# Cross-attention of a two-block kernel: softmax with queries on partitions before the transposes, in place of sums by products with ones after them

## The chip, the cores and the metric

The kernel runs on one core of one Trainium2 chip. The metric is the device time of one execution in microseconds (us); the times of a kernel are given as the median of its runs. The engines are called PE (TensorE, with PEld for its weight loads), DVE (VectorE), ACT (ScalarE), POOL (GpSimd) and SP (SyncE, which issues most DMAs). Each works through its own queue in order.

## The reference

Two transformer blocks run one after the other on x of 2 batches x 1024 tokens x 256 features, in float32. Both have self-attention over the 1024 tokens, then cross-attention over a context of 64 rows per batch, then a feed-forward part: in the first block a mixture of 8 experts of which each token uses 2, in the second a plain one. There are 16 heads of 16 features. The part that matters here is cross-attention, the same in both blocks but for biases and a mask:

```python
q = heads(norm(x) @ q_w.T)            # 1024 queries of a batch, 16 heads
k = heads(context @ k_w.T)            # 64 keys
v = heads(context @ v_w.T)
scores = einsum('bhqd,bhkd->bhqk', q, k) * 0.25   # block 2 adds a bias by the mask
attn = softmax(scores, axis=-1)
out = merge(einsum('bhqk,bhkd->bhqd', attn, v))
x = x + out @ proj_w.T
```

## The kernel before, in words

**Stages.** Each block (layer 0 and 1) begins with the first batch's norm and heads, then runs 128 *cells* (the loop at L954): one cell computes 4 tiles of scores for the maxima ahead (kind "a", L801, reduced by DVE at L808) and 4 tiles of scores again with the maxima folded in (kind "b", L812, exponentiated by ACT at L818), and every second cell multiplies the exponentials by the values (L863), which ACT copies (L875) and POOL adds up (L876). Eight PSUM banks go round for everything on PE: `bank()` (L230) takes the one that has been free longest, and a matmul waits until the bank's earlier reader is done. In the last 10 cells there are no more "a" scores; the flag `maxima[0]` then turns False, and `helper()` (L310) gives DVE in place of POOL.

**The order of the work.** A `Stream` (L131) holds all the other work as generators: norms, projections, cross-attention, the experts' dispatch and slots. Every task yields its estimated PE time in us, or zero or a negative number: wait until the next cell, or for that many us. In the cells `step` takes the able task with the earliest deadline and then the highest rank, as far as a budget of us for the cell goes. After the cells `rest` (L178) plays the remaining tasks against these estimates: the highest rank that isn't waiting goes next. All this happens while the program is written; on the chip the order is fixed on each engine.

**Cross-attention.** For each of 4 *units* of 512 queries in a layer, 8 in all, `cross_tasks` (L1071) adds three tasks: a norm (rank 67 or 40), `weigh` (rank 30, estimated at 17 us) and `share` (rank 50), which projects the result and adds it to x. The next unit's norm waits for this unit's `weigh`. `weigh` (L1098) first projects the queries (L1108). Its unit has 2 groups g of 8 heads, each of 4 tiles r; a tile holds 2 heads for the 512 queries: 128 queries on partitions, and along the free axis 4 such blocks of queries, each with 2 heads x 64 keys. Its steps are:

- `scores` (SC, L1123), two tiles at once: PE products (L1138; in layer 1 also the mask's, L1129). With `maxima` on, ACT copies the tile to SBUF (L1149); else DVE takes the maximum over each 64 keys (L1158) and subtracts it (L1159) straight from PSUM.
- `largest` (LA, L1164), with `maxima` on: the maximum by DVE (L1158) and the subtraction by POOL (L1159) in SBUF.
- `weights_turned` (TU, L1168), two tiles: 4 transposes each on PE (L1174), then Exp by ACT from PSUM to SBUF (L1178). From here on keys are on partitions.
- `product` (PR, L1184), once per g: the values' products (L1187), then 16 small products with ones, held in `picks` at O_SUM (L1197), which give the sums over keys; ACT copies the values' result (L1204) and DVE inverts the sums (L1206).
- `divided` (DI, L1209): 4 products with `picks` at O_HEAD spread the inverses over the features (L1212), and DVE multiplies (L1219). For g = 1 this is done in `share`, between waits of 2.6 and 1.2 us.

The order of these steps is written out by hand, once for units within the cells (L1227, 11 steps with a yield of 0.0 after each while `maxima` is on) and once for units after them (L1250, waits in us). A unit that begins within the cells keeps the first list, with its own waits once `maxima` is off.

**What goes on around the tails.** A unit of layer 0 is followed by a dispatch task (rank 70), which routes its tokens to experts and writes them to DRAM; `find` and `rows` then make the numbers of the experts' 20 slots, and `Mixture.slot` (rank 10 less the slot's number, estimated at 14.4 us) runs a slot's two matrix products with Gelu (L1657) between. Slot 0 can run after two units, slots 1 to 4 after the third, the others after the fourth. At the end of layer 0's cells the pools of its self-attention are closed and, in their place on the right side of SBUF, pools are opened in this order: `kpool`, `slotw` (slots' weights), `epool` 0 and 1 (slots' activations). Layer 1's beginning runs beside the slots (`beside`, L1981). After layer 1's cells, `forward_task` (rank 0, 28 us for each of 4 blocks, Gelu at L1814) runs in what the cross-attention leaves.

Of the kernel before, what the change touches and what calls it, by code (L numbers as in the profile page):

```python
# [106 lines left out]
O_SUM, O_HEAD = 0, 128  # L107

O_ROWS, O_PART = 640, 704
NPICK = 768  # L110
# [91 lines left out]
def two_blocks(  # L202
# [100 lines left out]
    def other_constants():  # L303
        nc.gpsimd.memset(restart, 1.0)
        nc.gpsimd.memset(restart[:, :, 0:1], 0.0)
        nc.gpsimd.memset(vbds[0], 0.0)

# [214 lines left out]
    def self_attention(layer, tail, heads, arrive, extra, when_ready, beside=None):  # L522
# [379 lines left out]
        if layer == 0:  # L902
            norm_pairs(0, TB, ln, x_turned(0), f"{names}0", arrive)

            one = small.tile([P, 1], F32, tag="one", name="one", bufs=1)
            nc.vector.tensor_copy(one, cols[:, C_ONE : C_ONE + 1])
            fill_heads(range(NK), one)
            other_constants()
            prepare()
            for i in range(2):  # L910
                spread_bias(i)
            for _ in first_heads():
                pass
# [184 lines left out]
    def weigh(layer, b, pool, w, name, held):  # L1098
# [68 lines left out]

        def weights_turned(g, n):  # L1168

            for r in (2 * n, 2 * n + 1):  # L1170
                i, p = bank()
                sc = less.pop((g, r))
                for t in range(4):
                    nc.tensor.transpose(  # L1174
                        p[:, t * P : (t + 1) * P], sc[:, t * P : (t + 1) * P], ident
                    )
                pt = pts[g, r] = pool.tile([P, 512], F32, tag="p1", name=f"pt_{name}{g}{r}", bufs=4)
                nc.scalar.activation(pt, p, AF.Exp, scale=SCALE)  # L1178
                free.append(i)


        inverse = {}

        def product(g):  # L1184
# [9 lines left out]
            j, s = bank()  # L1194
            for r in range(4):
                for c in range(4):
                    nc.tensor.matmul(  # L1197
                        s[32 * c : 32 * (c + 1), :P],
                        lhsT=picks[:, O_SUM + 32 * r : O_SUM + 32 * (r + 1)],
                        rhs=pts[g, r][:, c * P : (c + 1) * P],  # L1200
                        start=(r == 0),
                        stop=(r == 3),
                    )
            nc.scalar.copy(q[:, g, :], o)  # L1204
            inv = inverse[g] = pool.tile([P, P], F32, tag="inv", name=f"inv_{name}{g}", bufs=2)
            nc.vector.reciprocal(inv, s[:, :P])  # L1206
            free.extend((i, j))

        def divided(g):  # L1209
            i, p = bank()  # L1210
            for c in range(4):
                nc.tensor.matmul(  # L1212
                    p[:, c * P : (c + 1) * P],
                    lhsT=picks[:, O_HEAD + c * P : O_HEAD + (c + 1) * P],
                    rhs=inverse[g],
                    start=True,
                    stop=True,
                )
            nc.vector.tensor_tensor(q[:, g, :], q[:, g, :], p, ALU.mult)  # L1219
            free.append(i)  # L1220

        held.update(ot=q, divided=divided)
        cost = 1.9 if layer else 1.0
        SC, LA, TU, PR, DI = scores, largest, weights_turned, product, divided
        if maxima[0]:

            for now, wait in (  # L1227
                (((SC, 0, 0), (LA, 0, 0)), 0.0),
                (((LA, 0, 1),), 0.0),
                (((SC, 0, 1), (LA, 0, 2)), 0.0),  # L1230
                (((TU, 0, 0), (LA, 0, 3)), 0.0),
                (((SC, 1, 0), (LA, 1, 0)), 0.0),
                (((TU, 0, 1), (LA, 1, 1)), 0.0),
                (((SC, 1, 1), (LA, 1, 2)), 0.0),
                (((PR, 0), (LA, 1, 3)), -1.5),
                (((TU, 1, 0),), None),
                (((DI, 0), (TU, 1, 1)), -1.4),
# [4 lines left out]
                us = sum({SC: cost, TU: 1.15, PR: 1.1, DI: 0.55}.get(step[0], 0.0) for step in now)  # L1242
# [7 lines left out]
        for step, *args, wait in (  # L1250
            (SC, 0, 0, None),
            (SC, 0, 1, -1.0),
            (TU, 0, 0, None),
            (SC, 1, 0, None),
            (TU, 0, 1, -1.3),
            (PR, 0, None),
            (SC, 1, 1, None),
            (TU, 1, 0, None),
            (DI, 0, None),
            (TU, 1, 1, -1.6),  # L1260
            (PR, 1, None),
        ):
            step(*args)
            yield {SC: cost, TU: 1.15, PR: 1.1, DI: 0.55}[step]
# [716 lines left out]
    def beside(begin):  # L1981
# [4 lines left out]
        both.rest({}, 0)  # L1986
        mixture.others()
# [18 lines left out]
def _layout(inputs):  # L2006
# [84 lines left out]
    for r in range(4):  # L2091
        for u in range(2):
            for c in range(4):
                picks[SK * u : SK * (u + 1), O_SUM + 32 * r + 8 * c + 2 * r + u] = 1.0
# [52 lines left out]
```

## Time and profile before

| what | value |
|---|---|
| median of 3 runs | 1614.07 us (1609.81 to 1619.12) |
| the profiled execution: time | 1624.94 us |
| its span, first to last instruction | 1623.2 us |
| mean granted PE clock | 0.985 of full speed |
| Exp and Gelu table loads on ACT | 12, and one of another function at the start, 1283 ns each |

The profile is of one execution. Its page gives each engine's busy time, the chain of work that ended last, followed back from the end, and groups of like instructions by source line. Its windows give busy time by stretch of the span: layer 0's cells run from about 80 to 590 us, the experts' slots to about 950, layer 1's cells to about 1465, and the last feed-forward blocks to the end. An L with a number is a line of the kernel before. PE busy times are from modelled ends, so that neighbours seem to overlap by about 0.1 us.

### The profile page before, as it was taken

How to read it: one execution, taken by the hardware profiler on the slowest of the kernel's cores; microseconds unless marked ns; L12 is line 12 of the kernel's file. 1: busy time of each engine (PE TensorE's matmuls, PEld its weight loads, DVE VectorE, ACT ScalarE, POOL GpSimd, SP SyncE). 2: the span in 40 equal slices, each digit the busy share in tenths (PEclk: the TensorE clock that was granted, in tenths of full speed). 3: DMA queues.
4: the chain of work that ended last, by engine and by line, in shares of the span. 5: the costliest groups of instructions: out<-in, count | busy, mean ns of one | idle time of the engine just before them, and what ended most of it. 6: DMA issues, size and time to landing. Idle time of an engine off the chain costs nothing.

```text
span 1623.2 us, 28319 instructions
## 1 busy us (share of the span) xinstructions
PE 1579.5 (97%) x10710; PEld 876.8 (54%) x10710; DVE 985.1 (61%) x2094; ACT 912.9 (56%) x1767; POOL 411.0 (25%) x546
## 2 busy tenths in 40 slices
PE   7999999999998999999999999999999999999998
PEld 3433444544443547878888653344344435546766
DVE  5787776687778647511114457876867767855400
ACT  3487777676665755332233327876776676674321
POOL 2243323144235202311112032411322323311000
PEclk9899999999998999999999999999999999999999
DMA  5235311101000115375556321101110002000000
GB/s 158 112 133 194 111 27 34 28 21 47 14 21 34 54 50 196 102 275 188 186 201 217 92 72 27 33 23 21 34 33 21 22 14 83 15 14 21 14 13 26
DMA packets 55751, 121.07 MB, mean 75 GB/s; under 512 B 12218, under 2 KB 26428, under 8 KB 55228
## 3 DMA queue, kind: packets, MB, share of 16 engines
q1 hardware_dynamic: 51772, 109.07, 20.7%
q0 software_dynamic: 3456, 9.51, 1.6%
q8 instruction: 86, 1.41, 0.4%
q10 hardware_dynamic: 384, 0.66, 0.2%
q14 instruction: 53, 0.43, 0.1%
HBM read 71.68 MB, written 38.88 MB: 68 GB/s over the span
## 4 chain that ended last, share of the span: by engine, by line
PE 89%; DVE 7%; ACT 1%; issue 1%; DMA 1%; another core or an unknown queue 1%; POOL 0%; SPq 0%; DVEq 0%; POOLq 0%; ACTq 0%
PE banks L812 16%; PE banks L801 14%; PE banks L863 13%; PE banks L1651 8%; PE banks L1681 8%; PE banks L631 4%; PE banks L433 3%; PE banks L1823 3%; PE banks L1811 3%; DVE mx_s L808 3%; PE banks L1138 2%; PE banks L601 2%; PE banks L1174 2%; PE banks L1108 2%; PE banks L365 2%; PE banks L709 1%
## 5 line engine op out<-in xcount | busy, mean ns | idle before, releaser
L808 DVE TENSOR_REDUCE mx_s<-banks 128x1 f32<-128x512 f32 x1024 | 634.7, 682 | 215.3 <-PE banks L801 210.3
L818 ACT ACTIVATE pt_s<-banks 128x512 f32<-128x512 f32 x1024 | 532.6, 609 | 155.7 <-PE banks L801 124.8
L801 PE MATMUL banks<-KS,QS 16*128 16x512 f32 x2048 | 537.4, 631 | 4.0 <-DVE count L1441 2.6
L812 PE MATMUL banks<-qb_s,KS 32*128 32x512 f32 x2048 | 517.6, 623 | 6.7 <-DVE qb_s L711 3.7
L876 POOL TENSOR_TENSOR acc_s<-acc_s,part_s 128x512 f32<-128x512 f32 x141 | 179.5, 1273 | 439.0 <-ACT part_s L875 438.3
L812 PEld LDWEIGHTS banks<-qb_s,KS 32*128 32x128 f32 x2048 | 181.0, 187 | 178.5 <-DVE mx_s L808 105.4
L863 PE MATMUL banks<-pt_s,v_s 128*20 128x512 f32 x2048 | 262.0, 603 | 1.5 <-DVE mx_s L808 1.0
L801 PEld LDWEIGHTS banks<-KS,QS 16*128 16x128 f32 x2048 | 200.9, 186 | 76.3 <-issue 37.0
L1681 PE MATMUL banks<-w_slot,h_s 128*128 128x256 f32 x640 | 143.3, 380 | 2.7 <-ACT h_s L1657 2.7
L863 PEld LDWEIGHTS banks<-pt_s,v_s 128*20 128x20 f32 x2048 | 43.0, 98 | 185.0 <-ACT pt_s L818 131.6
L1681 PEld LDWEIGHTS banks<-w_slot,h_s 128*128 128x128 f32 x640 | 120.5, 190 | 22.8 <-ACT h_s L1657 3.1
L875 ACT COPY part_s<-banks 128x512 f32<-128x512 f32 x155 | 92.7, 598 | 61.3 <-PE banks L863 50.6
L1690 DVE SCALAR_TENSOR_TENSOR ys<-banks,gate,b 128x256 f32<-128x256 f32 x40 | 19.3, 483 | 170.3 <-PE banks L1681 163.3
L1657 ACT ACTIVATE h_s<-banks,w_slot 128x256 f32<-128x256 f32 x104 | 43.7, 471 | 109.0 <-issue 61.9
L1651 PE MATMUL banks<-xsT,w_slot 128*128 128x256 f32 x416 | 95.4, 381 | 0.7 <-ACT xsT L372 0.7
L1696 POOL DMA_INDIRECT results<-ys,to x40 | 38.8, 970 | 225.8 <-DVE ys L1690 183.3
L1651 PEld LDWEIGHTS banks<-xsT,w_slot 128*128 128x128 f32 x416 | 77.4, 190 | 14.9 <-DVE mx_s L808 2.3
L1159 POOL TENSOR_TENSOR sc_c<-sc_c,mx_c 128x512 f32<-128x512 f32 x38 | 40.0, 1054 | 98.8 <-DVE mx_c L1158 98.7
L631 PE MATMUL banks<-xT_s,w_att 128*128 128x512 f32 x128 | 63.9, 635 | 0.0
L1814 ACT ACTIVATE h_f<-banks,w_ff 128x512 f32<-128x512 f32 x32 | 22.0, 687 | 73.9 <-PE banks L1811 73.9
L1657 ACT ACTIVATE h_s<-banks,spare 128x256 f32<-128x256 f32 x56 | 23.3, 471 | 63.9 <-issue 30.4
L1823 PE MATMUL banks<-w_ff,h_f 128*128 128x256 f32 x256 | 57.3, 380 | 0.0
(270 smaller groups left out, 1647.2 us busy)
## 6 DMA issues: line engine op xcount, KB each, us to landing
w_slot<-in_ff_w_dram SPq DMA_DIRECT2D x40, 576.0 KB
sorted_rows<-fill SPq DMA_DIRECT2D x36, 520.0 KB
w_slot<-in_ff_w_dram SPq DMA_DIRECT2D x26, 514.0 KB
whole<-acc_s SPq DMA_DIRECT2D x30, 256.0 KB
spare<-in_ff_w_dram SPq DMA_DIRECT2D x14, 514.0 KB
xs<-sorted_rows SPq DMA_DIRECT2D x20, 260.0 KB
y<-results SPq DMA_DIRECT2D x16, 256.0 KB
QS<-stq_s SPq DMA_DIRECT2D x124, 32.0 KB
```

Source lines behind the costliest of these rows:

```text
L631: nc.tensor.matmul(p, lhsT=w[:, at + k * D + pair * P : at + k * D + (pair + 1) * P], rhs=xT[b][:, k, blk * 512 : (blk + 1) * 512], start= ...
L801: nc.tensor.matmul(sc, lhsT=QS[h % 4][r, qc * P : (qc + 1) * P], rhs=K[r, kh * 512 : (kh + 1) * 512], start=True, stop=True,)
L808: return i, lambda: nc.vector.tensor_reduce(mx[h][:, qc, j, kh : kh + 1], sc, AX.X, ALU.max)
L812: nc.tensor.matmul(sc, lhsT=K[r, n * P : (n + 1) * P], rhs=QB[h][r, :], start=True, stop=True)
L818: nc.scalar.activation(pt, sc, AF.Exp, scale=SCALE)
L863: nc.tensor.matmul(o[32 * j : 32 * j + VW, :], lhsT=V[b][:, cell % 8, 4 * g + j, :], rhs=exps.pop((cell, j)), start=(cell == cells[0]), st ...
L875: nc.scalar.copy(part, o)
L876: helper().tensor_tensor(acc[h], acc[h], part, ALU.add)
L1651: nc.tensor.matmul(ph[:, n, :], lhsT=w[:, at : at + P], rhs=xT[:, k, :], start=(k == 0), stop=(k == 1),)
L1657: nc.scalar.activation(h1[:, f, :], ph[:, n, :], AF.Gelu, bias=w[:, W_B1 + f : W_B1 + f + 1])
L1681: nc.tensor.matmul(py, lhsT=h1[:, f, h * P : (h + 1) * P], rhs=w[:, f * D : (f + 1) * D], start=(f == 0), stop=(f == 7),)
L1823: nc.tensor.matmul(py[:, n, :], lhsT=h1[:, f, t * P : (t + 1) * P], rhs=w2[:, f * D : (f + 1) * D], start=(f == 0), stop=(f == 7),)
```

## The change

The softmax is finished before the transposes, with queries on partitions and the 64 keys of a head along the free axis:

- A new step EX takes the Exp of one tile in place in SBUF, on ACT. A new step DI of one tile sums each 64 keys (DVE), inverts the 128x8 sums (DVE) and multiplies the tile by them (`helper()`: POOL in the cells, DVE after).
- TU now copies the transposed tile from PSUM by ACT, where it took the Exp.
- PR loses the 16 products with ones, the inversion and a bank; the old DI with its 4 spreading products per g and its multiplication is gone, in `share` too. The constants O_SUM in `picks` go.
- Both hand-written orders are new: 15 steps in the cells, and after them 13 entries with other waits. The cost estimates of the steps are 1.0 us (layer 0) or 1.9 us (layer 1) for SC, 1.15 for TU, 0.55 for PR.
- `ready_for_exp` issues an Exp of one column ahead of layer 0's cells and, in `beside`, after the slots and ahead of the branch for slots that are rarely needed.
- `slotw` is opened after the two `epool`s, so that the slots' weights and activations lie in another order in the place of the closed pools.

```diff
+    def ready_for_exp():
+
+        nc.scalar.activation(root, eps, AF.Exp)
...
             for _ in first_heads():
                 pass
+            ready_for_exp()
...
+        def exponentials(g, r):
+            nc.scalar.activation(less[g, r], less[g, r], AF.Exp, scale=SCALE)
+
+        def divided(g, r):
+
+            sc = less[g, r].rearrange("p (c k) -> p c k", k=SK)
+            sm = pool.tile([P, 8], F32, tag="smc", name=f"sm_{name}{g}{r}", bufs=4)
+            nc.vector.tensor_reduce(sm, sc, AX.X, ALU.add)
+            nc.vector.reciprocal(sm, sm)
+            helper().tensor_tensor(sc, sc, sm.unsqueeze(2).to_broadcast(shape), ALU.mult)
+
         def weights_turned(g, n):
...
-                nc.scalar.activation(pt, p, AF.Exp, scale=SCALE)
+                nc.scalar.copy(pt, p)
...
-            j, s = bank()
-            for r in range(4):
-                for c in range(4):
-                    nc.tensor.matmul(
-                        s[32 * c : 32 * (c + 1), :P],
-                        lhsT=picks[:, O_SUM + 32 * r : O_SUM + 32 * (r + 1)],
-                        rhs=pts[g, r][:, c * P : (c + 1) * P],
-                        start=(r == 0),
-                        stop=(r == 3),
-                    )
             nc.scalar.copy(q[:, g, :], o)
-            inv = inverse[g] = pool.tile([P, P], F32, tag="inv", name=f"inv_{name}{g}", bufs=2)
-            nc.vector.reciprocal(inv, s[:, :P])
-            free.extend((i, j))
-
-        def divided(g):
-            i, p = bank()
-            for c in range(4):
-                nc.tensor.matmul(
-                    p[:, c * P : (c + 1) * P],
-                    lhsT=picks[:, O_HEAD + c * P : O_HEAD + (c + 1) * P],
-                    rhs=inverse[g],
-                    start=True,
-                    stop=True,
-                )
-            nc.vector.tensor_tensor(q[:, g, :], q[:, g, :], p, ALU.mult)
             free.append(i)
...
-                (((SC, 0, 1), (LA, 0, 2)), 0.0),
-                (((TU, 0, 0), (LA, 0, 3)), 0.0),
-                (((SC, 1, 0), (LA, 1, 0)), 0.0),
+                (((SC, 0, 1), (LA, 0, 2), (EX, 0, 0)), 0.0),
+                (((LA, 0, 3), (EX, 0, 1), (DI, 0, 0)), 0.0),
+                (((EX, 0, 2), (DI, 0, 1)), 0.0),
+                (((TU, 0, 0), (EX, 0, 3), (DI, 0, 2)), 0.0),
+                (((SC, 1, 0), (LA, 1, 0), (DI, 0, 3)), 0.0),
                 (((TU, 0, 1), (LA, 1, 1)), 0.0),
-                (((SC, 1, 1), (LA, 1, 2)), 0.0),
-                (((PR, 0), (LA, 1, 3)), -1.5),
-                (((TU, 1, 0),), None),
-                (((DI, 0), (TU, 1, 1)), -1.4),
+                (((SC, 1, 1), (LA, 1, 2), (EX, 1, 0)), 0.0),
+                (((PR, 0), (LA, 1, 3), (EX, 1, 1), (DI, 1, 0)), 0.0),
+                (((EX, 1, 2), (DI, 1, 1)), -1.2),
+                (((TU, 1, 0), (EX, 1, 3), (DI, 1, 2)), -1.2),
+                (((DI, 1, 3),), -2.0),
+                (((TU, 1, 1),), -1.0),
                 (((PR, 1),), None),
...
-        for step, *args, wait in (
-            (SC, 0, 0, None),
-            (SC, 0, 1, -1.0),
-            (TU, 0, 0, None),
-            (SC, 1, 0, None),
-            (TU, 0, 1, -1.3),
-            (PR, 0, None),
-            (SC, 1, 1, None),
-            (TU, 1, 0, None),
-            (DI, 0, None),
-            (TU, 1, 1, -1.6),
-            (PR, 1, None),
+        for now, wait in (
+            (((SC, 0, 0),), None),
+            (((SC, 0, 1),), -2.0),
+            (((EX, 0, 0), (EX, 0, 1)), -1.2),
+            (((DI, 0, 0), (DI, 0, 1), (EX, 0, 2), (EX, 0, 3)), -2.4),
+            (((TU, 0, 0), (DI, 0, 2), (DI, 0, 3)), None),
+            (((SC, 1, 0),), -1.6),
+            (((TU, 0, 1),), -1.0),
+            (((SC, 1, 1), (PR, 0)), -1.6),
+            (((EX, 1, 0), (EX, 1, 1)), -1.2),
+            (((DI, 1, 0), (DI, 1, 1), (EX, 1, 2), (EX, 1, 3)), -2.4),
+            (((TU, 1, 0), (DI, 1, 2), (DI, 1, 3)), -2.6),
+            (((TU, 1, 1),), -1.6),
+            (((PR, 1),), None),
...
     def share(w, name, first, held):
 
-        yield -2.6
-        held["divided"](1)
-        yield 0.55
-        yield -1.2
+        yield -1.4
...
-    slotw.append(slots.enter_context(tc.tile_pool(name="slotw", bufs=2, side="right")))
+
     for n in range(2):
         epool.append(
             slots.enter_context(tc.tile_pool(name=f"epool{n}", bufs=2 - n, side="right"))
         )
+    slotw.append(slots.enter_context(tc.tile_pool(name="slotw", bufs=2, side="right")))
...
         both.rest({}, 0)
+        ready_for_exp()
         mixture.others()
```

More of the change, by code (lines that the diff above doesn't have):

```diff
@@ L104 @@
 NCOL = 139
-O_SUM, O_HEAD = 0, 128
-O_ROWS, O_PART = 640, 704
-NPICK = 768
+O_HEAD = 0
+O_ROWS, O_PART = 512, 576
+NPICK = 640
 W_O, W_V, W_Q, W_K = 0, 512, 1024, 1536
@@ L1177, in weights_turned @@
                 pt = pts[g, r] = pool.tile([P, 512], F32, tag="p1", name=f"pt_{name}{g}{r}", bufs=4)
-                nc.scalar.activation(pt, p, AF.Exp, scale=SCALE)
+                nc.scalar.copy(pt, p)
                 free.append(i)
-        inverse = {}
         def product(g):
@@ L1193, in product @@
                 )
-            j, s = bank()
-            for r in range(4):
-                for c in range(4):
-                    nc.tensor.matmul(
-                        s[32 * c : 32 * (c + 1), :P],
-                        lhsT=picks[:, O_SUM + 32 * r : O_SUM + 32 * (r + 1)],
-                        rhs=pts[g, r][:, c * P : (c + 1) * P],
-                        start=(r == 0),
-                        stop=(r == 3),
-                    )
-            nc.scalar.copy(q[:, g, :], o)
-            inv = inverse[g] = pool.tile([P, P], F32, tag="inv", name=f"inv_{name}{g}", bufs=2)
-            nc.vector.reciprocal(inv, s[:, :P])
-            free.extend((i, j))
-        def divided(g):
-            i, p = bank()
-            for c in range(4):
-                nc.tensor.matmul(
-                    p[:, c * P : (c + 1) * P],
-                    lhsT=picks[:, O_HEAD + c * P : O_HEAD + (c + 1) * P],
-                    rhs=inverse[g],
-                    start=True,
-                    stop=True,
-                )
-            nc.vector.tensor_tensor(q[:, g, :], q[:, g, :], p, ALU.mult)
-            free.append(i)
-        held.update(ot=q, divided=divided)
-        cost = 1.9 if layer else 1.0
-        SC, LA, TU, PR, DI = scores, largest, weights_turned, product, divided
+            nc.scalar.copy(q[:, g, :], o)
+            free.append(i)
+        held.update(ot=q)
+        costs = {scores: 1.9 if layer else 1.0, weights_turned: 1.15, product: 0.55}
+        SC, LA, EX, DI, TU, PR = (
+            scores, largest, exponentials, divided, weights_turned, product
+        )
         if maxima[0]:
@@ L1241, in weigh @@
                     step(*args)
-                us = sum({SC: cost, TU: 1.15, PR: 1.1, DI: 0.55}.get(step[0], 0.0) for step in now)
+                us = sum(costs.get(step, 0.0) for step, *_ in now)
                 if us:
@@ L1249, in weigh @@
             return
-        for step, *args, wait in (
-            (SC, 0, 0, None),
-            (SC, 0, 1, -1.0),
-            (TU, 0, 0, None),
-            (SC, 1, 0, None),
-            (TU, 0, 1, -1.3),
-            (PR, 0, None),
-            (SC, 1, 1, None),
-            (TU, 1, 0, None),
-            (DI, 0, None),
-            (TU, 1, 1, -1.6),
-            (PR, 1, None),
-        ):
-            step(*args)
-            yield {SC: cost, TU: 1.15, PR: 1.1, DI: 0.55}[step]
+        for now, wait in (
[12 more added lines that the diff above has]
+            (((PR, 1),), None),
+        ):
+            for step, *args in now:
+                step(*args)
+            us = sum(costs.get(step, 0.0) for step, *_ in now)
+            if us:
+                yield us
             if wait:
@@ L2090, in _layout @@
     picks = np.zeros((P, NPICK), f32)
[L2091 to L2094, printed above, removed]
     for j in range(4):
```

## The prediction

> **What bounds the kernel now.** I read the page's busy times first, then the chain of work that ended last, then busy time by stage, then the groups that the change touches, and last the timeline of one cross-attention unit. The page, busy time by engine and shares of the chain:
>
> ```profile
> PE 1579.5 (97%) x10710; PEld 876.8 (54%) x10710; DVE 985.1 (61%) x2094; ACT 912.9 (56%) x1767; POOL 411.0 (25%) x546
> ...
> PE 89%; DVE 7%; ACT 1%; issue 1%; DMA 1%; another core or an unknown queue 1%; POOL 0%; SPq 0%; DVEq 0%; POOLq 0%; ACTq 0%
> ```
>
> TensorE (PE) is busy nearly throughout, and nine tenths of the chain is its work. A busy PE could still be a slow one, so I ask by stage: layer 0's cells, its tail, layer 1's cells, the stretch with layer 1's last two units, and one unit alone (columns: stretch, length, then busy us of PE, PEld, DVE, ACT, POOL, then clock, DMA share, GB/s).
>
> ```profile
> 80.00:545.00 465.00, 457.33 (x3391) 200.18 (x3385) 352.84 (x686) 323.43 (x623) 164.06 (x208) 0.98 0.18 59
> 545.00:720.00 175.00, 165.11 (x1087) 116.38 (x1082) 95.91 (x334) 85.39 (x169) 40.87 (x43) 0.98 0.39 133
> 956.00:1428.00 472.00, 467.61 (x3644) 208.81 (x3644) 347.36 (x611) 332.39 (x638) 135.13 (x169) 0.99 0.12 33
> 1428.00:1545.00 117.00, 113.81 (x887) 71.96 (x884) 55.60 (x120) 56.53 (x101) 14.85 (x47) 1.00 0.05 15
> 256.00:308.00 52.00, 52.00 (x453) 26.13 (x453) 35.05 (x59) 37.28 (x72) 17.00 (x15) 1.00 0.11 22
> ```
>
> PE idles 7.7 us of 465 in layer 0's cells and not at all in the 52 us of a unit; ACT is at 72% there and DVE at 67%. Only layer 0's tail (545 to 720) shows real gaps, 9.9 us. The groups concerned (line, engine, shapes, count | busy us, mean ns | idle before):
>
> ```profile
> L1197 PE MATMUL banks<-pt_c,picks 128*32 128x128 f32 x512 | 17.7, 273 | 0.0
> L1212 PE MATMUL banks<-inv_c,picks 128*128 128x128 f32 x128 | 17.6, 280 | 0.3 <-DVE inv_c L1206 0.2 <-DVE mx_s L808 0.2
> ...
> L1178 ACT ACTIVATE pt_c<-banks 128x512 f32<-128x512 f32 x64 | 35.4, 612 | 22.1 <-PE banks L1174 21.5 <-ACT pt_c L1178 0.6
> ...
> L1158 DVE TENSOR_REDUCE mx_c<-sc_c 128x8 f32<-128x512 f32 x38 | 25.6, 673 | 14.7 <-ACT sc_c L1149 14.6
> ...
> L1159 POOL TENSOR_TENSOR sc_c<-sc_c,mx_c 128x512 f32<-128x512 f32 x38 | 40.0, 1054 | 98.8 <-DVE mx_c L1158 98.7
> ```
>
> There are 8 units of 8 score tiles each; 38 of the 64 tiles take the path in the cells (POOL subtracts), that is 4.75 units, and 26 the path outside. L1197 are the products with ones, L1212 those that spread the inverse; together 16 groups of each. What one group really takes on PE is the step from its start to that of the next work in the timeline:
>
> ```profile
> 293.99 1.06 PE L1197 MATMUL banks<-pt_c,picks 128*32 128x128 f32 x32
> 294.98 0.70 PE L812 MATMUL banks<-qb_s,KS 32*128 32x512 f32 x2
> ...
> 302.77 1.06 PE L1212 MATMUL banks<-inv_c,picks 128*128 128x128 f32 x8
> 303.67 1.04 PE L1174 MATMUL banks<-ident,sc_c 128*128 128x128 f32 x8
> ```
>
> 0.99 us and 0.90 us, with no gap before or after.
>
> [...] 32 instructions of 32 columns take the 1.06 us that 8 of 128 columns take, so the ones-products are already cheap, and their count of 512 says little. [...] the trace has every load at 1283 ns, and Exp and Gelu need different ones (loads at 1511.3 and 1527.2). [...] at 627.05 a DVE product of 64 elements (L1499) lasted 2.00 us, until a POOL addition ended at 628.96, where a like one (L1484) took 0.22.
>
> **The change, part by part.** *Removed from PE*: 16 x 0.99 + 16 x 0.90 = 30.2 us. The groups' own busy times add to 35.3, but count overlap with neighbours; in the chain a group has about 0.88, giving 28.2. I take 30, bounds 28 and 35. PE is the bound nearly everywhere, so this counts in full. Transposes and value products stay.
>
> *ACT*: a tile had one Exp (612 ns), and gets an Exp in SBUF and a copy. The Exp from SBUF isn't in the trace; nearest are L818's 609 ns from PSUM and the 602 of copies. I take 0.61, ends 0.5 and 0.8. Per unit 8 x 0.6 = 4.8 us more, 39 us in all. In layer 0's cells, with about 2.4 units, ACT goes from 323 to 335 of some 456 us (73%): covered by PE. Uncovered, if each new Exp delayed the drains queued behind it (self-attention's L818, whose banks PE waits for), the 38 in the cells would cost 23 us.
>
> *DVE*: per unit 8 sums (as L1158, 0.67) and 8 reciprocals of 128x8 (between 178 ns for 128x4 and 339 for 128x32: 0.2) = 7.0, less 2 reciprocals of 0.958 and 2 products of 0.683 = 3.3: 3.7 us more. Outside the cells also 8 products on DVE (0.69, as L876 there): 9.2 more. In the cells 353 + 9 = 362 us, 79%: still covered. *POOL* in the cells: 8 x 1.05 = 8.4 us per unit, 164 to 184 us: covered, if not punctual.
>
> *New waits.* In the cells an Exp waits on ACT for POOL's subtraction issued two steps before; a sum waits on DVE for the Exp one step before, with mx_s maxima (L808) behind it; a transpose waits on PE for POOL's product, often only one step old, with everything of PE behind it. A step is a cell, 465/128 = 3.6 us or more. From sum to product takes 0.67 + 0.2 + 1.05 = 1.9 us, plus up to one POOL addition ahead (1.27, L876): 3.2. So most waits are met, some by little. The trace shows no such wait; its bounds are nothing and 3.2 us for each of the 19 transposing steps in the cells (61 us). I take about 1 us per unit, 5 us. The unit takes 15 steps where it took 11, so it ends some four cells later, and the dispatch of layer 0's third unit with it.
>
> *Layer 0's tail.* DVE's own work on unit 3 grows from 8 x 1.37 = 11 to about 24 us. Scores started at 628.8 and the last products at 645.4; the unit becomes some 9 us longer. Cover is experts' slots 1 to 4, whose weights were sent for from 621.6 to 633.4. The rows of slot 5 were asked for at 697.4 and used at 715.6, 18 us later: that slack takes the 9 us, and perhaps the Exp/Gelu switches, two loads (2.6 us) each time a slot's Gelus fall between groups of Exps. I take 4 us lost, ends 0 and 18. *Layer 1's tail*: same lengthening and the same switches, under up to 28 us of feed-forward per block as cover (PE idle 3.2 of 117): 3 us lost, ends 0 and 10.
>
> *The early Exp* (`ready_for_exp`): in layer 0 the load sat at 49.2, the first Exp at 53.6: nothing. In layer 1 it came at 954.3 after the branch, and PE waited 2.9 us for the Exps: up to 1.3 gained, or nothing if the branch makes a second load necessary. I take 1. *The slots' tiles*: the weight load at 590.1 had waited 33.0 us at the head of SP's queue for the last self-attention product, with the context's loads behind it (591.0). Their users start at 598.6 and 613.9 without a wait for them, so an earlier place gains nothing visible; a later one than 590.1 isn't possible, since that product is the last user of the old pools. I take 0, with 6 us either way for the ACT gap of 6.1 us at 622 that the trace doesn't explain.
>
> **Sum.** -30 - 1 + 5 + 4 + 3 = -19 us, against the profiled execution's own 1624.9 us (span 1623.2 and 1.7 around it): 1606, or -1.2%. That execution lies 0.7% above the median of 1614.07; the same share of the median gives 1595 us.
>
> **The rivals.** *ACT's order makes it slower.* Each of the 38 Exps in the cells stands ahead of the next cell's drains; if it shows in full and waits half a subtraction more, (0.61 + 0.53) x 38 = 43 us, net +13: 1627. It decides against the change from 0.8 us per Exp (30/38), and beyond 0.5% from 1.0. For it: PE's loads for L863 waited 63.7 us, in 82 waits, on ACT in layer 0's cells. Against: those waits lie under running matmuls, PE idle being 7.7 us, and the Exp gets two cells. *The gain is given back outside the cells.* If layer 0's tail uses up its slack and loses 18, layer 1's loses 5: -30 + 23 + 1 for the cells = -6: 1608. For it: the tail has PE's only gaps, and DVE's chain doubles. Against: slots are ready to be pulled forward. *All cover holds*: -30 to -35: 1579 to 1584. That the products don't vanish is excluded: the diff deletes them.
>
> **How the numbers follow.** A change of 0.5% is about what a measurement of this kernel can tell from none: below 1606, above 1622. Forecast with the full-cover case 0.75 (1580 to 1606); given back in the tails, or partly in the cells, 0.13 (to 1622); ACT's order 0.12 (1627). The range runs from 1580 to 1611: it leaves out the slower case, half of the middle one and the lowest 0.02.
>
> **What would show it.** Right: L1197 and L1212 gone, PE's busy time down by about 30 us, its idle in the cells up by 5 or less, ACT at about 950 us. Wrong: idle PE before transposes released by POOL or DVE, over 3 us a unit; ACT idle before SBUF Exps, released by POOL; gaps over 20 us between 620 and 720; more than six or so extra table loads in the units after the cells.

## The result, and the profile after

The change makes the kernel slower, by about two thirds of a per cent: 1625.85 us median (1621.85 to 1628.86) against 1615.52 for the kernel before on the same chip (1609.81 to 1619.12), a ratio of 1.0064, 95% interval [1.0043, 1.0085]. Forecast was 1.2% faster. A repetition on another chip (after_again) gave 1.0036 [1.0023, 1.005]. The first series below was run where the kernel before took 1616.29 us; the later ones were run on three other chips, called A, B and C, where it took 1631.20, 1631.29 and 1631.51 us, about 1% longer. So kernels are compared by their ratio to the kernel before on the same chip. Lengths of stages are compared within one chip; where that is not possible, the text says so.

An L with a number is from here on a line of the changed kernel: L1174 is the new Exp, L1180 to L1182 are the division's sum, reciprocal and multiplication, L1190 the transposes, L1194 their copies. From the page, busy time by engine and the shares of the chain that ended last:

```profile
PE 1560.5 (96%) x10070; PEld 850.1 (52%) x10070; DVE 1034.8 (64%) x2237; ACT 961.7 (59%) x1851; POOL 449.5 (28%) x572
...
PE 37%; DVE 2%; POOL 1%; ACT 1%; issue 0%; DMA 0%; DVEq 0%; POOLq 0%; ACTq 0%
```

PE has lost 640 instructions (320 small products, each of which is two instructions in the trace), but its busy time fell by only 19 us (1579.5 to 1560.5), not by 30, and its idle time (span less busy) grew from 43.7 to 63.6 us: what busy time fell came back as idle time, one for one. (The chain of this profile stops early, so its shares of the span are not those of before; it still names PE.) The same stretches as before the change, in the same columns:

```profile
80.00:545.00 465.00, 454.37 (x3278) 195.24 (x3272) 361.30 (x717) 337.85 (x653) 185.80 (x229) 0.97 0.18 60
545.00:720.00 175.00, 154.39 (x868) 110.84 (x869) 108.13 (x363) 88.69 (x172) 36.65 (x39) 0.96 0.39 133
956.00:1428.00 472.00, 464.12 (x3496) 197.23 (x3492) 355.18 (x634) 344.04 (x661) 154.50 (x177) 0.99 0.11 32
1428.00:1545.00 117.00, 109.73 (x679) 64.96 (x676) 64.81 (x150) 67.50 (x113) 11.38 (x32) 0.94 0.05 15
256.00:308.00 52.00, 52.00 (x403) 23.91 (x400) 40.08 (x72) 41.34 (x81) 25.13 (x23) 1.00 0.11 22
```

PE's idle time rises in each but the last: 7.7 to 10.6 us, 9.9 to 20.6, 4.4 to 7.9, 3.2 to 7.3. The second thing to see is the clock, third number from the right: 0.98 to 0.96 in layer 0's tail, 1.00 to 0.94 in layer 1's. The single unit at 256 to 308, whose timeline the prediction rests on, shows nothing of either. The groups of the new steps (busy us, mean ns | idle us ahead of them, and who ended it):

```profile
L1174 ACT ACTIVATE sc_c<-sc_c 128x512 f32<-128x512 f32 x64 | 39.7, 639 | 3.9 <-DVE sc_c L1164 3.8
L1180 DVE TENSOR_REDUCE sm_c<-sc_c 128x8 f32<-128x512 f32 x64 | 43.3, 676 | 12.3 <-ACT sc_c L1174 12.3
L1181 DVE RECIPROCAL sm_c<-sm_c 128x8 f32<-128x8 f32 x64 | 13.0, 203 | 2.2
L1182 POOL TENSOR_TENSOR sc_c<-sc_c,sm_c 128x512 f32<-128x512 f32 x34 | 35.8, 1053 | 14.4 <-DVE sm_c L1181 14.4
L1182 DVE TENSOR_TENSOR sc_c<-sc_c,sm_c 128x512 f32<-128x512 f32 x30 | 20.8, 692 | 1.0
...
L1190 PE MATMUL banks<-ident,sc_c 128*128 128x128 f32 x256 | 40.3, 298 | 29.9 <-DVE sc_c L1182 16.2 <-POOL sc_c L1182 13.7
```

The durations are within 5% of the estimate (0.61, 0.67, 0.2, 1.05, 0.69 us). The last line is the loss: PE stood idle for 29.9 us ahead of transposes, 13.7 for POOL's multiplication and 16.2 for DVE's, where the kernel before, whose transposes are its L1174, had 1.7:

```profile
L1174 PE MATMUL banks<-ident,sc_c 128*128 128x128 f32 x256 | 34.8, 277 | 1.7 <-DVE sc_c L1159 1.7
```

Of the 29.9 us, 15.5 lie in units that begin in the cells, 14.4 in the units after them. One of the places, layer 0's second unit, in order of time (start, length, engine):

```profile
395.42 0.20 DVE L1181 RECIPROCAL sm_c<-sm_c 128x8 f32<-128x8 f32 x1
...
398.44 1.01 POOL L1421 DMA_INDIRECT sorted_rows<-xd_m,at_m  x1 [0.16 <-issue]
...
398.81 0.20 DVE L1181 RECIPROCAL sm_c<-sm_c 128x8 f32<-128x8 f32 x1
...
399.75 0.97 POOL L1421 DMA_INDIRECT sorted_rows<-xd_m,at_m  x1 [0.30 <-issue]
...
400.75 1.05 POOL L1164 TENSOR_TENSOR sc_c<-sc_c,mx_c 128x512 f32<-128x512 f32 x1
...
401.75 1.27 POOL L880 TENSOR_TENSOR acc_s<-acc_s,part_s 128x512 f32<-128x512 f32 x1
...
402.97 1.04 POOL L1182 TENSOR_TENSOR sc_c<-sc_c,sm_c 128x512 f32<-128x512 f32 x1
404.06 1.12 PE L1190 MATMUL banks<-ident,sc_c 128*128 128x128 f32 x4 [3.27 <-POOL sc_c L1182]
...
407.69 1.05 POOL L1182 TENSOR_TENSOR sc_c<-sc_c,sm_c 128x512 f32<-128x512 f32 x1
...
408.79 1.12 PE L1190 MATMUL banks<-ident,sc_c 128*128 128x128 f32 x4 [3.62 <-POOL sc_c L1182]
409.84 1.22 PE L816 MATMUL banks<-qb_s,KS 32*128 32x512 f32 x2
```

POOL's queue is full. The inverses for the first two multiplications were ready at 395.6 and 399.0 us, but POOL took the multiplications up at 402.97 and 407.69: ahead of the first it had three of the dispatch's indirect DMAs to issue (about 1.3 us from one to the next), and a subtraction and two additions to do. Two gaps of 3.27 and 3.62 us result. The last row shows what follows: a pair of scores takes 1.22 us where a pair took 0.66 at 398. The PE clock (third number from the right) in that stretch, of the kernel after and then of the kernel before:

```profile
400.00:420.00 20.00, 13.12 (x72) 7.14 (x72) 9.20 (x18) 7.70 (x14) 12.47 (x12) 0.58 0.07 27
```

```profile
400.00:420.00 20.00, 20.00 (x168) 10.33 (x160) 14.35 (x25) 14.21 (x28) 8.80 (x8) 1.00 0.04 14
```

0.58 is half clock for 17 of 20 us; in windows of 1 us the clock goes to 0.50 at 403.3, within the first gap, and back to 1.00 at 420.4, nearly 12 us after the second. PE was busy without a pause from 409.84 us on, and half clock lasted 10.5 us more. Such a gap can thus cost a second time, and my sum had no term for that. It is not the only occasion: the kernel before has half clock (0.50) from 139.1 to 142.5 us with no gap of 2 us near it (the nearest, ahead of 138.17, is 1.04 us).

Layer 0's last unit, outside the cells:

```profile
619.59 1.72 PE L1143 MATMUL banks<-kbd,q_c 32*128 32x128 f32 x32
620.85 0.69 DVE L1163 TENSOR_REDUCE mx_c<-banks 128x8 f32<-128x512 f32 x1 [1.42 <-PE banks L1143]
621.24 1.99 PE L1058 MATMUL banks<-w_ctx,kvT 128*128 128x256 f32 x8
...
626.86 0.63 ACT L1174 ACTIVATE sc_c<-sc_c 128x512 f32<-128x512 f32 x1 [0.69 <-DVE sc_c L1164]
628.19 0.17 DVE L1519 TENSOR_TENSOR tiles<-tiles,tiles 128x8 f32<-128x8 f32 x1
628.28 0.68 DVE L1180 TENSOR_REDUCE sm_c<-sc_c 128x8 f32<-128x512 f32 x1
...
629.22 0.69 DVE L1182 TENSOR_TENSOR sc_c<-sc_c,sm_c 128x512 f32<-128x512 f32 x1
...
630.06 1.09 PE L1190 MATMUL banks<-ident,sc_c 128*128 128x128 f32 x4 [6.83 <-DVE sc_c L1182]
```

From the scores to the first transpose 10.5 us pass: four maxima and subtractions on DVE, with the small operations of `find` between them and behind them (to 628.4), then the first division. PE finds 2 us of other work (the context, L1058) and then none: the next slot's rows were only asked for at 631.3.

### The profile page after: what moved, and what is told of

Its sections match the earlier page's. It is cut to its first block, busy times and chain, and to the rows that moved or that the text cites. A ratio compares the mean times of both kernels' runs of the same rounds, so it can differ in the third digit from the quotient of the medians.

```text
span 1624.1 us, 27275 instructions
## 1 busy us (share of the span) xinstructions
PE 1560.5 (96%) x10070; PEld 850.1 (52%) x10070; DVE 1034.8 (64%) x2237; ACT 961.7 (59%) x1851; POOL 449.5 (28%) x572
## 5 line engine op out<-in xcount | busy, mean ns | idle before, releaser
L812 DVE TENSOR_REDUCE mx_s<-banks 128x1 f32<-128x512 f32 x1024 | 633.7, 680 | 215.0 <-PE banks L805 212.2
L816 PE MATMUL banks<-qb_s,KS 32*128 32x512 f32 x2048 | 523.0, 630 | 5.2 <-DVE qb_s L715 2.7
L880 POOL TENSOR_TENSOR acc_s<-acc_s,part_s 128x512 f32<-128x512 f32 x149 | 189.2, 1270 | 394.7 <-ACT part_s L879 392.1
L867 PE MATMUL banks<-pt_s,v_s 128*20 128x512 f32 x2048 | 265.4, 607 | 0.0
L879 ACT COPY part_s<-banks 128x512 f32<-128x512 f32 x164 | 98.8, 602 | 56.1 <-PE banks L867 43.2
L1693 POOL DMA_INDIRECT results<-ys,to x40 | 38.7, 968 | 247.6 <-DVE ys L1687 205.9
L1190 PE MATMUL banks<-ident,sc_c 128*128 128x128 f32 x256 | 40.3, 298 | 29.9 <-DVE sc_c L1182 16.2
L1808 PE MATMUL banks<-hT_f,w_ff 128*128 128x512 f32 x128 | 59.2, 611 | 0.0
```

Source lines behind the costliest of these rows:

```text
L812: return i, lambda: nc.vector.tensor_reduce(mx[h][:, qc, j, kh : kh + 1], sc, AX.X, ALU.max)
L816: nc.tensor.matmul(sc, lhsT=K[r, n * P : (n + 1) * P], rhs=QB[h][r, :], start=True, stop=True)
L867: nc.tensor.matmul(o[32 * j : 32 * j + VW, :], lhsT=V[b][:, cell % 8, 4 * g + j, :], rhs=exps.pop((cell, j)), start=(cell == cells[0]), st ...
L879: nc.scalar.copy(part, o)
L880: helper().tensor_tensor(acc[h], acc[h], part, ALU.add)
L1808: nc.tensor.matmul(ph, lhsT=w1[:, at : at + P], rhs=hT[:, k, :], start=(k == 0), stop=(k == 1))
```

## The experiments

Two tables first, from each profile: the time at which PE reached five marks, given as lengths (us): to the first value product of layer 0's self-attention; on to layer 0's last unit's query projection; on to the last slot's first transposes; on to layer 1's first value product; on to PE's end. The diffs are abridged: words in them stand for code. First series:

| kernel | start | layer 0's cells | its tail and slots | to layer 1 | layer 1 | PE's end |
|---|---|---|---|---|---|---|
| before | 66.8 | 555.6 | 277.8 | 69.9 | 648.8 | 1618.9 |
| after | 64.2 | 551.9 | 281.6 | 65.6 | 656.5 | 1619.8 |
| no_division | 64.3 | 541.1 | 282.0 | 65.4 | 638.8 | 1591.6 |
| before_no_ones | 66.5 | 547.5 | 268.3 | 70.0 | 636.0 | 1588.3 |
| dve_divides | 64.2 | 544.0 | 283.6 | 65.6 | 663.7 | 1621.1 |

(The profiled execution of before was 0.7% above its median, so its row is rather long.) Later series, with the chip:

| kernel, chip | start | layer 0's cells | its tail and slots | to layer 1 | layer 1 | PE's end |
|---|---|---|---|---|---|---|
| before_new_places, A | 64.5 | 562.2 | 279.3 | 65.2 | 650.4 | 1621.6 |
| after_again, B | 66.4 | 557.2 | 286.3 | 65.6 | 657.2 | 1632.7 |
| later_turn, B | 66.6 | 548.2 | 295.1 | 65.6 | 645.3 | 1620.8 |
| first_only, A | 67.2 | 550.8 | 283.7 | 65.6 | 649.3 | 1616.6 |
| combined, C | 66.9 | 554.3 | 283.2 | 65.6 | 644.9 | 1614.9 |

**The removed products alone.** The kernel before without them; inverses, their spreading and the multiplication are left out too, so nothing is divided.

```diff
-            j, s = bank()
-            for r in range(4): ... products with picks[:, O_SUM ...]
...
         def divided(g):
-            ... products with picks[:, O_HEAD ...], multiplication
+            pass
```

> The kernel before in its own order, with the products with ones, the inverses, the spreading products and the multiplication left out (weights not normalised). It prices what the change takes off PE. Late divisions: 30 us of PE work on the path, 1580 to 1588 us. Rival, the products were hidden behind other engines: over 1600 us.

Measured: 1590.2 us (1586.76 to 1594.34), ratio 0.9821 [0.9797, 0.9844], 29 us, 2 us short of the range expected. The products were on the path, at the price forecast.

**The division alone.** The changed kernel without it.

```diff
         def divided(g, r):
-            ... sum, reciprocal, multiplication
+            pass
```

> The changed kernel with the step DI left out: no sums, no inverses, no multiplication (so the attention weights are not normalised); all Exps, copies and transposes stay in their places. Late divisions (PE waits at its transposes for the product by the inverses, 29.9 us in the profile after, and its clock is halved for a while after the long waits, about 15 us more than before): both go, PE keeps the 30 us of products removed, so some 1583 to 1592 us. Rival, the added Exps on ACT or the longer lists: the loss stays, 1615 to 1625 us.

Measured: 1597.64 us (1597.44 to 1598.94), ratio 0.9876 [0.9855, 0.9896]. The division costs 28 us (30 by the ratios), about the whole gain of 29, though its sums, reciprocals and products lie on DVE and POOL. But 20 us below the kernel before is not the 23 to 33 expected: some 9 us remain, for which Exps, table loads and the longer lists are candidates; no run separates them. In the table they seem to sit in layer 0's tail, which is no shorter than after (282.0), while before_no_ones saved 9.5 us there.

**Who multiplies.**

```diff
-            helper().tensor_tensor(sc, sc, ..., ALU.mult)
+            nc.vector.tensor_tensor(sc, sc, ..., ALU.mult)
```

> The changed kernel with the multiplication of DI always on DVE, in the cells too. Late divisions: the 13.7 us of waits for POOL's product in the cells go, and with them the half-speed stretch of 17 us after 404 us (8 us lost) and that after 1348: 1605 to 1612 us. Rival, DVE is too full in the cells (38 x 0.69 = 26 us more, maxima late): 1625 us or more.

Measured: 1625.0 us (1622.41 to 1627.29), ratio 1.0044 [1.0027, 1.006]: no gain, as the rival had it, though the gaps at 404 and 409 are gone, with most of their half clock (400 to 420 in this kernel):

```profile
400.00:420.00 20.00, 20.00 (x149) 10.54 (x152) 17.15 (x29) 14.33 (x30) 12.48 (x11) 0.92 0.15 48
```

Layer 0's cells became 8 us shorter and layer 1 7 us longer: there DVE's maxima for self-attention (L812) now stand behind the multiplications, and PE waits for them, 0.3 to 1.4 us at a time. These waits (5.7 us in all in layer 1's cells, where POOL's multiplication had cost 4.6) and 6.8 us of half clock at 1212 explain a part of the 7 us; the rest is open. POOL was the worse engine in one stage and DVE in the other.

**The two small parts.** Undone in the changed kernel, and alone in the kernel before:

```diff
-            ready_for_exp()
...
-    for n in range(2):
-        epool.append(...)
     slotw.append(...)
+    for n in range(2):
+        epool.append(...)
```

> The changed kernel with the order of the slots' pools as before and without the early Exp. Late divisions: these two parts carry nothing, 1623 to 1628 us. Rival, the places or the early Exp cost: 1610 to 1620 us.

> The kernel before with the two small parts of the change alone: the early Exp at both places and the slots' weights opened after their activations. Theory A (these two parts gain by themselves, as their undoing cost 4 to 7 us in the changed kernel): ratio to before 0.996 to 0.9975, that is 1609 to 1612. Theory B (they only gain where the softmax is done early, since the prediction gave them 1 us): 0.999 to 1.001, 1614 to 1617.

Measured: 1.0088 [1.0058, 1.0119] undone, 0.9989 [0.9976, 1.0002] alone. The first lies outside both of its expectations and had looked like a gain of 4 us and more that I had missed, but its interval meets that of the change (1.0064), and alone the two parts give about 2 us, by the interval anything from 0 to 4. The 1 us of the forecast lies in it. The stage on to layer 1 is 4.3 us shorter after (65.6 against 69.9), and as short with the two parts alone (65.2, chip A): PE's gap of 2.91 us at 956 and the 6.8 us of half clock that begin in it are gone. Why the whole kernel gains less than this is open.

**Cells or tails.** First the division left out only after the cells:

```diff
         def divided(g, r):
+            if not maxima[0]:
+                return
```

> The changed kernel with the sums, the inverses and the multiplication left out once the cells have ended, so that these units' softmax is not divided; in the cells it is. All of the division costs 28 us. Theory A (most of that is paid in the units after the cells, where nothing covers DVE's chain): 1602 to 1610. Theory B (most is paid in the cells, and the tails lose by the longer list and by the Exps instead): 1613 to 1620.

Measured: 0.9974 [0.9961, 0.9988]. Between the two: against 1.0036 for the change (on chip B; this is chip A) it saves 10 us, about a third of what all of the division costs. Then the new scheme only where a unit begins in the cells, in both layers, and only in layer 0 with DVE:

```diff
+        early = maxima[0]                     # old_outside
+        early = maxima[0] and layer == 0      # first_only, nc.vector multiplies
...
+                if early: copy, else Exp; sums by products only if not early
```

> The new scheme only for the units that begin in the cells (layer 0's first three, layer 1's first two), with the division on POOL as in the changed kernel; the other three units as before; with the early Exp and the new places of the slots' tiles. Theory A (the new scheme is worth having in the cells and is lost in the units after them): 5 units x 3.8 us of PE saved, less some 8 of waits, less 5 for the places: 1598 to 1607. Theory B (its waits take the gain in the cells as well): not better than the two small parts alone, 1609 to 1617.

> As the last, but the new scheme only for layer 0's first three units, and their division on DVE at once. Theory A (in layer 0's cells the scheme gains once POOL's queue is out of the way): 3 x 3.8 us less, waits of 1 to 3, places 5: 1600 to 1606. Theory B (what the cells gain moves into layer 0's tail, because the third unit ends later and the slots with it): 1609 to 1616.

Measured: 1.0003 [0.9988, 1.0019] and 0.9952 [0.9938, 0.9966], the second between its two theories. For old_outside theory A fell: in the cells as they stand the scheme gains nothing over the small parts alone (0.9989). By the stages layer 0 gained 3.2 us over the small parts alone and layer 1 lost 3.5 (653.9 against 650.4): there two units save 7.6 us of PE, but a gap of 3.56 us at 1353 and one of 0.88 at 1400 appear, and half clock for 6.8 us. Where POOL is out of the way, in first_only, three units gain 0.4%, 6 us. By the ratios it is faster than both kernels.

**Too late by one cell.** The transposes one step later, no work added or removed:

```diff
-                (((TU, 0, 0), (EX, 0, 3), (DI, 0, 2)), 0.0),
-                (((SC, 1, 0), (LA, 1, 0), (DI, 0, 3)), 0.0),
+                (((EX, 0, 3), (DI, 0, 2)), 0.0),
+                (((TU, 0, 0), (DI, 0, 3)), 0.0),
+                (((SC, 1, 0), (LA, 1, 0)), 0.0),
...
-                (((TU, 1, 0), (EX, 1, 3), (DI, 1, 2)), -1.2),
-                (((DI, 1, 3),), -2.0),
+                (((EX, 1, 3), (DI, 1, 2)), -1.2),
+                (((TU, 1, 0), (DI, 1, 3)), -2.0),
+                ((), -1.0),
                 (((TU, 1, 1),), -1.0),
```

> The changed kernel once more, without an edit, so that the next three can be compared with it on one chip. Both theories: a ratio to before of 1.004 to 1.0085, as in its first runs.

> The changed kernel with the transposes in the cells' list one step later behind the division (17 steps in place of 15). Theory A (in the cells the products come too late by a part of one cell): the waits at 404, 409, 547, 555, 1348 and 1393 us (15.5 us) go, and the half-clock stretches after them (27 us, worth 13): at most 29 us, less 2 to 4 in the tails for the units' later ends; 1600 to 1612. Theory B (the waits of the cells move to other places, or the third unit's later end costs layer 0's tail as much): 1618 to 1628.

Measured: 1.0036 [1.0023, 1.005], just under its range, and 0.9953 [0.9939, 0.9968], a difference of 0.0083 or 13.5 us, as theory A had it. The transposes' group in later_turn:

```profile
L1190 PE MATMUL banks<-ident,sc_c 128*128 128x128 f32 x256 | 38.5, 292 | 10.7 <-DVE sc_c L1182 5.8 <-POOL sc_c L1182 1.7 <-POOL rs_f L327 0.8
```

and in after_again:

```profile
L1190 PE MATMUL banks<-ident,sc_c 128*128 128x128 f32 x256 | 40.1, 297 | 33.9 <-DVE sc_c L1182 19.5 <-POOL sc_c L1182 14.3 <-DVE mx_s L812 0.2
```

Waiting for POOL falls from 14.3 to 1.7 us, for DVE from 19.5 to 5.8. By the table, layer 1 gives 11.9 us. Layer 0's cells give 9.0, but its tail takes 8.8 back: with two more steps a unit ends later, and layer 0's tail has no room for that. Its last unit begins 8.8 us earlier, but the dispatch behind the third unit 1.1 us later (604.6 against 603.5).

**Half clock after a gap.** PE filled with unread products in the gap of layer 0's last unit. This gap was 6.83 us after the change and 11.84 us in after_again; each of the 14 products is two instructions, and together they took 13.2 us, not the 6.0 expected:

```diff
+            if layer == 0 and now[0] == (TU, 0, 0):
+                i, o = bank()
+                for _ in range(14):
+                    nc.tensor.matmul(o, lhsT=ident, rhs=xT[:, 0, :], start=True, stop=True)
+                free.append(i)
```

> The changed kernel with 14 products of 128x512 that nobody reads (about 6.0 us of PE at 0.43 each) put ahead of the first transposes of layer 0's last unit, in the place where PE stood idle for 6.83 us; the computation is whole. Theory A (idle gaps of PE of some us bring a stretch of half clock after them, which costs as much as the gap itself): the 10.2 us of half clock after that gap go, 4 to 6 us faster than the changed kernel: ratio to before about 1.003. Theory B (the half clock comes by itself, or from what else runs then): as the changed kernel, or up to 1 us slower.

Measured: 1.0023 [1.001, 1.0036] against 1.0036 [1.0023, 1.005] for the same kernel unfilled. The stretch behind the transposes, unfilled and then filled:

```profile
643.00:660.00 17.00, 16.53 (x98) 13.57 (x97) 13.33 (x36) 11.21 (x18) 0.00 (x0) 0.78 0.70 241
```

```profile
646.00:662.00 16.00, 15.16 (x109) 12.23 (x108) 12.90 (x34) 13.20 (x21) 0.00 (x0) 1.00 0.64 233
```

With useless work in the gap the clock behind it was 1.00, where it had been 0.78 (one profile of each). The price of the half clock is not shown: 0.0013 is 2 us, and the intervals overlap. From the queries' projection to the value products PE was 2 us faster, though the filling itself delayed the first transpose by 1.8; by the slots from 5 on 0.3 us was left.

**Layer 0's tail.** The last unit takes 24.0 us from its queries' projection to the end of its last value product before the change, 41.2 after it, and 41.5 without the division; in after_again it takes 45.8. Waits written into its list, or the chain?

```diff
-                yield wait
+                yield wait if layer == 1 else 0.3 * wait
```

> The changed kernel with the written waits of the list outside the cells cut to 0.3 of their length for layer 0's last unit alone (17.6 us of waits in its list become 5.3; the kernel before had 3.9). That unit took 40 us from its queries' projection to its last product where the kernel before took 23, and 40 to 43 also with the division left out. Theory A (the written waits, in which slots' products go first, make it long, and with it the dispatch that the slots from 5 on wait for): 25 to 32 us, and a ratio to before of 0.999 to 1.002. Theory B (the chain over ACT and DVE makes it long): PE stands idle in the place of the waits, and the ratio stays at 1.003 to 1.008.

Measured: 1.0072 [1.005, 1.0094], in theory B's range, and the unit took 42.7 us (chip C). My theory of the written waits fell: some 12 us of waits were cut, the unit is 3 us shorter than in after_again (chip B), and nothing is won end to end. The gap of 11.84 us ahead of the first transposes is the same in both. Neither leaving out the division nor cutting the waits brings the unit near its old length; that either is long enough to hold it alone is a reading of this, not shown, since no run leaves out both. Two hybrids with the old last unit and 17 steps in the cells:

```diff
+        early = maxima[0]                     # both_cells, DVE multiplies in layer 0
+        early = maxima[0] or layer == 1       # later_old_tail0, helper() multiplies
```

> The new scheme for the units that begin in the cells of both layers, with the transposes one step later as in the last kernel, the division on DVE in layer 0 and on POOL in layer 1; the units after the cells as before; the early Exp and the new places. Theory A (with punctual divisions layer 1's two units save their 3.8 us each as well): 7 us below the version with layer 0's three units alone, ratio to before 0.989 to 0.993. Theory B (in layer 1's cells the new scheme has nothing to give): 0.994 to 0.998.

> The changed kernel with the transposes one step later in the cells (which gave 0.9953), and layer 0's last unit alone done as before the change. Theory A (that unit costs the scheme 4 to 9 us in layer 0's tail): 0.990 to 0.993. Theory B (with 17 steps the third unit and the dispatch behind it end so late that no slot is there to cover the last unit, as in the version with both cells): 0.996 to 1.004.

Measured: 1.0108 [1.0078, 1.0138] and 0.9989 [0.9976, 1.0003], both misses of theory A; the first is outside theory B as well. In both, layer 0's tail and slots are long: 300.2 us (chip B) and 298.8 (chip C), against 286.3 in after_again. The kernel both_cells lost in other stages too: its layer 0's cells took 560.8 us and its layer 1 655.7 (548.2 and 645.3 in later_turn, same chip); in the cells PE waited 2.27 us at 412 and 3.78 at 556 for DVE's maxima, in layer 1 the cause is open. In both_cells the dispatch of the third unit came at 616.8 instead of 603.5 (after_again), the second slot's rows at 668.9 instead of 649.0, and PE idled 5.4 us for them; in later_old_tail0 it idled 4.9 us for them. A last unit that is quick again is of little use when no slot stands ready beside it: the lateness of the third unit is a cost of its own.

**What the stages ask for, put together.** Layer 0: the change's 15 steps, DVE multiplies, the last unit as before. Layer 1: the new scheme throughout, transposes one step later.

```diff
+        early = maxima[0] or layer == 1
+            if maxima[0] and layer == 0: the change's 15 steps
+            elif maxima[0]: the 17 steps of later_turn
...
+            (nc.vector if layer == 0 else helper()).tensor_tensor(sc, sc, ..., ALU.mult)
```

> In layer 0 the new scheme for the three units of the cells, in the change's own 15 steps with the division on DVE, and the last unit as before; in layer 1 the new scheme throughout, in the cells with the transposes one step later. Theory A (the gain of layer 0's part, 0.9963 of the kernel with the small parts alone, and of layer 1's, 12 us, are in different stages and add): 0.989 to 0.993. Theory B (what one stage gains the next gives back): 0.994 to 0.998.

Measured: 1620.14 us (1616.86 to 1624.38) against 1631.51 for before on that chip, ratio 0.9935 [0.9913, 0.9957]: between the theories, and faster than both kernels, by about 11 us than before and, by the ratios, 16 than the change. From its page the busy times, then the transposes' group:

```profile
PE 1572.5 (97%) x10150; PEld 858.4 (53%) x10150; DVE 1040.8 (64%) x2237; ACT 951.0 (59%) x1837; POOL 430.8 (27%) x550
```

```profile
L1190 PE MATMUL banks<-ident,sc_c 128*128 128x128 f32 x256 | 38.9, 294 | 7.9 <-DVE sc_c L1182 3.1 <-DVE mx_c L1164 2.3 <-POOL rs_f L327 0.8
```

The transposes' waits are down to 7.9 us. The gains of the two layers do not quite add (0.9952 for layer 0's part, and 12 us less in layer 1, would give 0.988 or so): layer 1 took 644.9 (chip C) where first_only took 649.3 (chip A), since 7 of the 12 us only made good what the change had lost there (657.2 on chip B against 650.4 in before_new_places).

## Why the prediction was wrong, by its own steps

The forecast was 19 us faster; 10 us slower was measured.

*The products removed, 30 us*: right (29 measured). *The durations on ACT, DVE and POOL*: right. *ACT's order*, the rival to the other side: the sign came out, but not by this mechanism. It was to begin at 0.8 us for each Exp in the cells; ACT idled 3.9 us ahead of all 64, and leaving out the division alone takes away 30 of the 39 us that lie, by the ratios, between the change and before_no_ones. For the Exps at most the rest is left.

*New waits, "I take about 1 us per unit, 5 us"*: **this is the step that failed.** The bounds that I had written, 0 to 61 us, held the answer; the choice did not. I reckoned a division at 1.9 us, "plus up to one POOL addition ahead", against a step of 3.6, and concluded that most waits are met. But I priced POOL's queue by its mean load and one neighbour. From 391 to 406 us it had to issue eight DMAs of the dispatch as well, and the first multiplication stood 7.3 us in the queue; I had counted POOL's queue only for its share of busy time. Measured: 15.5 us of idle PE at the transposes of the cells' units where 5 were forecast, and 13.5 us won by one step's delay (later_turn, its half clock included). With the units after the cells it is 29.9 us, or 3.7 a unit: the sign that the prediction had named for being wrong. The sign it had named for being right, idle PE in the cells up by 5 or less, was met as well (7.7 to 10.6 us and 4.4 to 7.9): a PE at half clock counts as busy (all of 410 to 420 us, at a clock of 0.50), and other idle time shrank.

*No term for the clock*: at each gap of 3 us or more that the waits made, half clock set in, within the gap or up to 1.1 us behind it: for 17.1 us at 404 and 409 (3.27 and 3.62 us), 10.2 at 630 (6.83), 3.4 at 1348 (3.71), 10.2 at 1461 (3.06). Over the span the clock's loss (one less the clock, over all stretches) was 23.9 us before and 38.7 after. Not all of these 15 us are lost time, as PE idles in a part of them. PE was busy for 67.6 us of half clock after and 45.7 before; half of the difference is 11 us of longer work, an estimate for a clock of 0.50, and just what PE's busy time lacks of the 30 forecast (19 came). How much of it the kernel's time felt is not shown: where it could be tested, about 2 us of a 17 us stretch came back.

*Layer 0's tail, 4 us lost*: too small. The unit became 17 us longer, not 9; tail and slots took 3.8 us more, where the 3.8 us of one unit's products should have gone: 7.6 lost. The cover named there, slots 1 to 4, was not to be had where the unit needed it: slot 1's rows were asked for 15.2 us into the unit (631.3), when the gap of 6.83 us was over, where the kernel before had asked 8.4 us into it. The unit began 6.3 us earlier, but the dispatch behind the third unit came no earlier (595.9 against 596.0). That a unit ends later I had noted ("ends some four cells later") and not priced. *Layer 1's tail, 3 us*: with its cells, layer 1 took 7.7 us more where 15 should have gone (four units), so 23 were lost. About half is the cells' lateness (later_turn wins 11.9); gaps of 3.06 and 0.89 us at 1461 and half clock behind them are seen in the rest. The table loads, 24 where there were 13, are more than the forecast's limit of six or so; what they cost was not taken apart.

*The rival "given back outside the cells"* was nearest: its place is a part of the truth, as no_division_after saves 10 of the 28 us of the division there; but it had the cells give back 1 us, where a step's delay in their list alone won 13.5. *The slots' places and the early Exp, 1 us*: right within the interval.

Left open: why DVE stood idle for 5.4 us at 627 in after_again, and as long in filled, with the scores ready (the profile names no releaser on this core); this is most of what makes the gap 11.84 us there and 6.83 in the first profile. Also how the remaining 9 us of no_division divide among Exps, table loads and lists.

## What to carry to other kernels

Work taken off the bounding engine is worth its time only if what replaces it is punctual: for every new wait on that engine, look at the queue of the engine waited for at that place in the trace, DMA issues included, and not at its share of busy time. Where a hand-written order has a step's slack of less than that queue, move the reader a step later and check what its later end holds up. Try each stage by itself: the engine, the slack and the scheme that suit one loop may be wrong for the next.

## What the runs showed of the hardware

- With a PE gap of 3.27 us and one of 3.62 close behind it the clock was 0.50 for 17.1 us, from within the first gap (after); with another gap filled by products that nobody reads (filled) the clock behind it was 1.00, where it had been 0.78 (after_again). In the changed kernel's profile the stretches of half clock within the span last 3.4, 6.8, 10.2, 13.7 or 17.1 us, in all nine within 0.05 us of a multiple of 3.41. The rows of the changed kernel behind the second gap show it without any counter: 1.22 us for a pair of scores at 409.84 in place of 0.66 at 398.
- An indirect DMA held POOL's queue for about 1.3 us where another followed (0.96 to 1.01 and a pause of 0.30; after, 392 to 406 us), so that a row of them delayed what was queued behind by about as much as so many additions of 128x512 (1.27 us each).
